# Carrying four partial sums in HBM with GpSimd's accumulating transfers

## The chip, the cores and the metric

One Trainium2 chip, of which the program uses one core. The metric is the time of one execution on the device in microseconds (us). All data are float32.

## What is computed

Eight batch rows of 512 positions by 256 features pass through nine gated feed-forward blocks (eight experts with weights Wg, Wu, Wd and one shared block Sg, Su, Sd, each 256 to 1024 and back), and their weighted sum is added to the input:

```python
g = jnp.einsum('bsd,edf->ebsf', h, Wg)
u = jnp.einsum('bsd,edf->ebsf', h, Wu)
expert_outs = jnp.einsum('ebsf,efd->ebsd', jax.nn.silu(g) * u, Wd)
expert_output = jnp.einsum('be,ebsd->bsd', gating_probs, expert_outs)
shared = jnp.einsum('bsf,fd->bsd', jax.nn.silu(h @ Sg) * (h @ Su), Sd)
return x + (1.0 - sg) * expert_output + sg * shared
```

## The kernel before, in words

The work is cut into 36 units: two halves of the batch (four batch rows each), nine blocks e, and two groups g of 512 hidden features. A unit holds four tiles of 128 hidden features and four batch rows, and forms all 16 products (feature tile by batch row) of the gate, of the up-projection and, after them, of the down-projection. It does this with fewer matmuls than the plain way by a scheme of sums and differences of the four indices: `PAIRS` lists the six pairs (i, j), and for each pair the kernel builds differences and sums of weights (tiles u and wb, on GpSimd, lines 427 to 443) and of inputs (v and b, loaded from copies in HBM, lines 334 and 351).

A unit has two stretches. In the first, the hub, the four products with i = j are made (P and Q steps, lines 503 to 540); in the second, the block, the six pairs (R1 and R steps, lines 549 to 571). Each product ends in `finish` (line 487): ScalarE applies Silu to the gate, VectorE multiplies by the up-projection and the block's weight into a tile h. Tiles h live in a ring of 11 buffers.

The down-projection of a unit (`down`, line 605) is a generator that starts near the end of the unit's hub and runs on into the hub of the next unit; its matmuls are threaded between the gate and up matmuls by the strings at lines 907 to 913. It makes:

- for each pair p the products r (line 664), s or S (lines 672 to 679) and X (line 692). The pairs in `OWN` (0 to 3) have a sum of their own, S, which is carried over all units of a half, in the SBUF tile accS. `carried` (line 639) copies accS into the PSUM bank (`seeded`, line 633), lets TensorE accumulate the unit's matmul on top, and copies the bank back (line 642). Both copies are ScalarE's.
- at the unit that closes a half, no copy back: the seeded bank itself is subtracted from the result's accumulators (lines 674 to 681).
- four products p of row sums (tile rows) and four products q of column sums (tile cols). These sums of h are made by `add_sum` (line 589) on GpSimd: 32 parts a unit, of which the first of a sum adds two tiles, so 24 additions of 128x512 a unit. They are queued by pair in `h_sums` and given out one or two a step, in the block and in the next unit's hub; `flush_sums` (line 597) gives out what is missing just before the matmul that needs it.

The order of the instructions on TensorE and on GpSimd is that of the program text (`manual_schedule`, line 945); on ScalarE, VectorE and SyncE a scheduler sets it. Every engine runs its instructions in order. All DMA transfers are issued by SyncE, except the first loads, which ScalarE issues; GpSimd issues none. In units 2 to 17 a further generator, `prepare` (line 247), makes the second half's input forms: its subtractions and additions on GpSimd are lines 282 to 288 (tile f).

Of the kernel before, what the change touches and what calls it, by code (L numbers as in the profile page):

```python
# [10 lines left out]
F32 = mybir.dt.float32  # L11
AF = mybir.ActivationFunctionType
ALU = mybir.AluOpType
# [4 lines left out]
def kernel(  # L18
# [37 lines left out]
    nc = tc.nc  # L56
    B, S, D = x.shape
    E, _, F = Wg.shape
    P = 128
# [6 lines left out]
    PAIRS = ((1, 0), (0, 2), (3, 0), (1, 2), (3, 1), (3, 2))  # L66
# [17 lines left out]
    zpool = ctx.enter_context(tc.tile_pool(name="z", bufs=6))  # L84
    spool = ctx.enter_context(tc.tile_pool(name="s", bufs=4))
    dpool = ctx.enter_context(tc.tile_pool(name="d", bufs=2))
    iopool = ctx.enter_context(tc.tile_pool(name="io", bufs=2))
    dram = ctx.enter_context(
        tc.tile_pool(name="dram", bufs=1, space=bass.MemoryType.DRAM)
# [7 lines left out]
    gp = nc.gpsimd  # L97
# [25 lines left out]
    def issue_after(later, *first):  # L123

        for at in first:
            tc.add_manual_dep(
                later.ins,
                at.ins.name,
                mybir.DependencyInfo(
                    mybir.DependencyClass.NoSync, mybir.DependencyReason.DATA  # L130
                ),
                reason="issue order",
            )
# [6 lines left out]
    xdram = {}  # L140
    recent = {}
    latest_h = []

# [4 lines left out]
    def new_po(name, turns=False):  # L150

        k = po_next[0]
        if held[k]:
            k = 1 - k
        if not turns:
            po_next[0] = 1 - k
        return ps_o.tile([P, S], F32, tag=f"po{k}", name=name), k
# [223 lines left out]
    for h in range(NH):  # L381
        for e in range(NE):
            for g in range(GRP):
                u = Unit()
# [204 lines left out]
    def add_sum(u):  # L589
        which, n, at = u.sums.pop(0)  # L590
        sums = getattr(u, which)
        first = n not in sums
        if first:
            sums[n] = sumpool.tile([P, S], F32, tag="sum", name=f"{which}{n}_{u.name}")
        gp.tensor_tensor(sums[n], u.h_[n, n] if first else sums[n], u.h_[at], ALU.add)  # L595

    def flush_sums(u, which, n):
        while any(w == which and k == n for w, k, _ in u.sums):
            add_sum(u)

    def closes(u):

        return u.n + (2 if u.h + 1 == NH else 1) == len(units) * (u.h + 1) // NH

    def down(u, acc):

        def tile_of(key):
            acc[key] = apool.tile(
                [P, S], F32, tag=f"acc{key[0]}{key[1]}", name=f"acc{key[0]}{key[1]}_{u.h}"
            )  # L610
            return acc[key]

        def put(key, bank, s):

            if key not in acc:
                if s == 1.0:
                    nc.scalar.copy(tile_of(key), bank)
                else:
                    nc.scalar.mul(tile_of(key), bank, s)
            elif s == 1.0:  # L620
                return ve.tensor_add(acc[key], bank, acc[key])  # L621
            elif s == -1.0:
                return ve.tensor_sub(acc[key], acc[key], bank)
            else:
                return ve.scalar_tensor_tensor(acc[key], bank, s, acc[key], ALU.mult, ALU.add)

        def seeded(key, w, b):

            po, k = new_po(f"{key[0]}{key[1]}_{u.name}")
            full = key in acc and not turned[k]  # L630
            turned[k] = False
            if full:
                nc.scalar.copy(po, acc[key])  # L633
            nc.tensor.matmul(  # L634
                po, w, b, start=not full, stop=True, skip_group_check=full
            )
            return po, full

        def carried(key, w, b):
            po, full = seeded(key, w, b)  # L640
            if full:
                nc.scalar.copy(acc[key], po)
            else:
                put(key, po, 1.0)
            return po if full else acc[key]

        def carried_with(key, w, b, half, s):
            po, full = seeded(key, w, b)
            assert full
            ve.scalar_tensor_tensor(  # L650
                acc[key], xhub[u.h, key[1]][:, half], s, po, ALU.mult, ALU.add
            )

        def single(key, w, b):
            po, k = new_po(f"{key[0]}{key[1]}_{u.name}")
            turned[k] = False
            nc.tensor.matmul(po, w, b, start=True, stop=True)  # L657
            return po, k

        def pair(p):  # L660
            i, j = PAIRS[p]
            d = CI[i] - CI[j]
            def first():
                A, k = single(("r", p), u.Wd[p][i], u.h_[i, j])
                put(("B", j), A, 1.0)
                held[k] = True
                return A, k

            def second():
                args = u.Wd[p][j], u.h_[j, i]  # L670
                if p in OWN and not closes(u):
                    carried(("S", p), *args)
                    return
                if p in OWN:
                    o, full = seeded(("S", p), *args)
                    if not full:
                        ve.tensor_add(o, o, acc["S", p])
                else:
                    o, _ = single(("s", p), *args)
                put(("B", i), o, -1.0)  # L680
                put(("V", p), o, -1.0)

            if closes(u) and p < SWAPPED:
                second()
                yield
                A, k = first()
            else:
                A, k = first()
                yield
                second()  # L690
            yield
            nc.tensor.matmul(  # L692
                A, u.Ud[p], u.X[p], start=False, stop=True, skip_group_check=True
            )
            if closes(u):
                made = ve.tensor_add(A, A, acc["V", p])
                if latest_h[0] is u:
                    issue_after(made, latest_h[1])
                u.puts = put(("b", i), A, 1.0 / d), put(("b", j), A, -1.0 / d)
            else:  # L700
                put(("V", p), A, 1.0)
            held[k] = False
            po_next[0] = 1 - k
            yield

        done = {}
        for what in (0, 1, 2, 3, 4, "p0", "q0", 5, "q1", "p1", "q2", "p2", "q3", "p3"):
            if isinstance(what, int):
                yield from pair(what)
                continue  # L710
            i = int(what[1])
            extra = carry_on.get(u.n)
            if extra is not None and extra[0] == what:
                flush_sums(u, "rows" if what[0] == "p" else "cols", i)
                if what[0] == "p":
                    key, w, b = ("b", i), u.raw_d[:, i, 0:P], u.rows[i]
                else:
                    key, w, b = ("B", i), u.ad[i], u.cols[i]
                carried_with(key, w, b, *extra[1:])
            elif what[0] == "p":  # L720
                flush_sums(u, "rows", i)
                done[what] = carried(("b", i), u.raw_d[:, i, 0:P], u.rows[i])
            else:
                flush_sums(u, "cols", i)
                po, _ = single(("q", i), u.ad[i], u.cols[i])
                put(("B", i), po, 1.0)
                done[what] = po
            if closes(u) and f"p{i}" in done and f"q{i}" in done:
                if CI[i] != 0.0:
                    put(("B", i), done[f"p{i}"], -CI[i])  # L730
                for r in (0, 1):
                    ends[u.h, i, r] = acc["bB"[r], i]
            yield
# [78 lines left out]
    def gate_up(u, nxt):  # L812
# [12 lines left out]
        if u.n == 1:  # L825
            for _ in range(2):
                add_sum(units[0])
# [138 lines left out]
    behind, acc, ahead = iter(()), {}, prepare(1)  # L966
    for u in units:
# [6 lines left out]
        for what in FIRST if u.n == 0 else LAST if nxt is None else OPENING if u.opens else ORDER:  # L974
            if what == "G":
                if nG == TAKE:
                    for _ in behind:
                        pass
                    if u.opens:
                        acc = {}  # L980
                    behind = down(u, acc) if nxt is not None else iter(())
# [7 lines left out]
                if nG > TAKE and nG % 2 == 0 and u.sums:  # L989
                    add_sum(u)  # L990
# [67 lines left out]
```

## Time and profile before

| | us |
|---|---|
| two runs, median (lowest to highest) | 2430.32 (2429.84 to 2430.8) |
| span of the profiled execution | 2427.7 |
| TensorE busy in it (share) | 2423.2 (100%) |
| GpSimd busy in it (share) | 2082.6 (86%) |
| VectorE busy in it (share) | 1919.5 (79%) |
| ScalarE busy in it (share) | 1239.0 (51%) |

Runs take 2.6 us more than the span of the profiled execution (2430.3 against 2427.7), which lies around the instructions of the program. In the rows, PE is TensorE's matmul, PEld its weight load, DVE VectorE, ACT ScalarE, POOL GpSimd and SP SyncE, with a q for the engine's own queue. A float32 matmul stands as two records, so that the timeline merges it as "x2". A row of the timeline gives the start, the length, engine, line, operation, written and read tiles; in square brackets the time that the engine had been idle, and what ended it. An issued DMA is not counted as busy time.

### The profile page before, as it was taken

Reading aid. Unit: us, or ns where it says so; the run is one execution under the profiler, and the core shown is the slowest. Engines: PE = TensorE matmul, PEld = TensorE weight load, DVE = VectorE, ACT = ScalarE, POOL = GpSimd, SP = SyncE. Lnnn points to the kernel's source line nnn. Section 1 sums busy time; section 2 is a strip of 40 time slices with the busy share of each in tenths; the row PEclk is TensorE's granted clock in tenths of the full one; section 3 lists DMA queues with packets and bytes.
Section 4 is the critical chain, followed back from the end, with each engine's and each line's share of the span. In section 5 each row is a group of like instructions: output and inputs, shape, how many; then the busy total and the mean of one; then the engine's idle time right before and its main releaser. Section 6 shows DMA issues by size and latency. Waiting matters only on the chain.

```text
span 2427.7 us, 22771 instructions
## 1 busy us (share of the span) xinstructions
PE 2423.2 (100%) x5735; PEld 1085.3 (45%) x5735; DVE 1919.5 (79%) x2861; ACT 1239.0 (51%) x2294; POOL 2082.6 (86%) x2321
## 2 busy tenths in 40 slices
PE   9999999999999999999999999999999999999999
PEld 4444444444444444444444444444444444444446
DVE  8788888777777877787987777777877777777795
ACT  5555555554555454555455555555455555555542
POOL 7988888898988989898888888888888888888882
PEclk9999999999999999999999999999999999999999
DMA  4333333334333332334453322322333333323245
GB/s 161 108 111 107 110 98 100 117 117 126 104 122 104 103 113 94 108 112 124 119 124 110 91 84 91 92 87 90 100 104 104 95 97 90 92 87 96 79 132 145
DMA packets 221201, 257.92 MB, mean 106 GB/s; under 512 B 64016, under 2 KB 156432, under 8 KB 221072
## 3 DMA queue, kind: packets, MB, share of 16 engines
q1 hardware_dynamic: 220240, 256.17, 35.4%
q8 instruction: 48, 0.79, 0.1%
q14 instruction: 81, 0.66, 0.1%
q10 hardware_dynamic: 832, 0.30, 0.0%
HBM read 238.59 MB, written 17.83 MB: 106 GB/s over the span
## 4 chain that ended last, share of the span: by engine, by line
PE 100%; DVE 0%; issue 0%
PE c L565 31%; PE c L552 15%; PE c L530 10%; PE c L506 10%; PE r L657 7%; PE r L692 7%; PE b L634 5%; PE S L634 5%; PE q L657 5%; PE s L657 2%; PE tail L792 1%; PE B L634 0%; PE ptx L234 0%; PE touchg L372 0%; PE c L212 0%; PE ptx L208 0%
## 5 line engine op out<-in xcount | busy, mean ns | idle before, releaser
L565 PE MATMUL c<-b,wb 128*128 128x512 f32 x1728 | 847.1, 592 | 0.0
L490 ACT ACTIVATE sg<-c 128x512 f32<-128x512 f32 x576 | 343.7, 597 | 571.1 <-DVE c L570 330.3
L495 DVE SCALAR_TENSOR_TENSOR h<-sg,coef,c 128x512 f32<-128x512 f32 x576 | 427.5, 742 | 240.7 <-PE c L565 133.9
L565 PEld LDWEIGHTS c<-b,wb 128*128 128x128 f32 x1728 | 328.2, 190 | 408.8 <-issue 388.2
L552 PE MATMUL c<-v,u 128*128 128x512 f32 x864 | 441.1, 592 | 0.0
L595 POOL TENSOR_TENSOR rows<-rows,h 128x512 f32<-128x512 f32 x280 | 369.4, 1319 | 0.0
L557 DVE TENSOR_TENSOR c<-D,c 128x512 f32<-128x512 f32 x432 | 298.8, 692 | 76.7 <-ACT sg L490 57.9
L595 POOL TENSOR_TENSOR cols<-cols,h 128x512 f32<-128x512 f32 x280 | 358.8, 1281 | 0.0
L570 DVE TENSOR_TENSOR c<-c,D 128x512 f32<-128x512 f32 x432 | 298.6, 691 | 21.7 <-PE c L565 21.2
L506 PE MATMUL c<-x,w 128*128 128x512 f32 x572 | 274.5, 592 | 0.0
L442 POOL TENSOR_TENSOR wb<-u,wb 128x256 f32<-128x256 f32 x108 | 79.5, 736 | 220.1 <-ACT wb L440 220.1
L552 PEld LDWEIGHTS c<-v,u 128*128 128x128 f32 x864 | 163.6, 190 | 206.1 <-issue 164.8
L657 PE MATMUL r<-h,wd 128*128 128x512 f32 x420 | 214.5, 592 | 0.0
L692 PE MATMUL r<-X,ud 128*128 128x512 f32 x420 | 214.5, 592 | 0.0
L530 PE MATMUL c<-x,at 128*128 128x512 f32 x432 | 208.7, 592 | 0.0
L540 ACT COPY D<-c 128x512 f32<-128x512 f32 x284 | 165.6, 584 | 84.1 <-DVE h L495 84.1
L581 DVE TENSOR_TENSOR X<-h,h 128x512 f32<-128x512 f32 x202 | 199.4, 987 | 6.8
L595 POOL TENSOR_TENSOR rows<-h,h 128x512 f32<-128x512 f32 x140 | 193.4, 1382 | 0.0
L595 POOL TENSOR_TENSOR cols<-h,h 128x512 f32<-128x512 f32 x140 | 180.5, 1289 | 0.0
L512 ACT COPY P<-c 128x512 f32<-128x512 f32 x216 | 126.1, 586 | 105.5 <-PE c L506 100.9
L506 PEld LDWEIGHTS c<-x,w 128*128 128x128 f32 x572 | 108.5, 190 | 135.8 <-issue 112.4
L633 ACT COPY S<-accS 128x512 f32<-128x512 f32 x132 | 77.9, 590 | 158.4 <-DVE accV L621 140.2
(115 smaller groups left out, 3470.5 us busy)
## 6 DMA issues: line engine op xcount, KB each, us to landing
b<-xs SPq DMA_DIRECT2D x210, 512.0 KB, 3.6
v<-xs SPq DMA_DIRECT2D x210, 256.0 KB, 2.6
wd<-in_L_cond_Wd_dram SPq DMA_DIRECT2D x32, 512.0 KB, 4.8
w<-in_L_cond_Wg_dram SPq DMA_DIRECT2D x127, 128.0 KB, 3.5
w<-in_L_cond_Wu_dram SPq DMA_DIRECT2D x127, 128.0 KB, 3.6
f<-xd SPq DMA_DIRECT2D x12, 512.0 KB, 5.3
xs<-f SPq DMA_DIRECT2D x18, 256.0 KB, 2.7
xin<-in_x_dram SPq DMA_DIRECT2D x16, 256.0 KB, 3.7
```

The costliest lines, as they stand in the source:

```text
L490: nc.scalar.activation(s, bank, AF.Silu)
L495: made = ve.scalar_tensor_tensor(t, u.sg[i, j], coef[:, u.e, b : b + 1], bank, ALU.mult, ALU.mult)
L506: nc.tensor.matmul(bank, u.raw[i][:, m, 0], xhub[u.h, i][:, 0], start=True, stop=True)
L530: nc.tensor.matmul(bank, u.at[i][:, m], xhub[u.h, i][:, 1], start=False, stop=True, skip_group_check=True,)
L552: nc.tensor.matmul(bank, u.U[p][:, m], u.V[p], start=False, stop=True, skip_group_check=True)
L557: made = ve.tensor_sub(other, u.Ds[j, m], bank)
L565: nc.tensor.matmul(bank, u.W[p][:, r, m], u.VB[p][:, r], start=False, stop=True, skip_group_check=True,)
L570: first_order(u, ve.tensor_add(bank, bank, u.Ds[j, m]), "add", p, m)
L595: gp.tensor_tensor(sums[n], u.h_[n, n] if first else sums[n], u.h_[at], ALU.add)
L634: nc.tensor.matmul(po, w, b, start=not full, stop=True, skip_group_check=full)
L657: nc.tensor.matmul(po, w, b, start=True, stop=True)
L692: nc.tensor.matmul(A, u.Ud[p], u.X[p], start=False, stop=True, skip_group_check=True)
```

## The change

Two things change, both on GpSimd's queue.

First, S of the pairs 0 to 3 is no longer carried in SBUF. The matmul starts its bank afresh, ScalarE copies the bank into a staging tile St (a ring of four), and a transfer adds it to a tile S in HBM: the first of a half is a plain store from SyncE, the others are transfers of GpSimd with `accum_op=ALU.add`, 256 KB each. The transfer is not issued at once but when the next of these sums is made (`parked`). In the unit that closes a half, each sum is loaded back into a staging tile, Sin, by SyncE, and seeds the bank as accS did.

Second, of the 24 additions of `add_sum` two become such transfers in SBUF: the additions of h to the row sums 1 and 2 at pair 3, in all units but the first.

```diff
+    stpool = ctx.enter_context(tc.tile_pool(name="st", bufs=4))
...
+        if not first and which == "rows" and at in (PAIRS[3], PAIRS[3][::-1]) and u.n:
+            gp.dma_start(sums[n], u.h_[at], accum_op=ALU.add)
+            return
         gp.tensor_tensor(sums[n], u.h_[n, n] if first else sums[n], u.h_[at], ALU.add)
...
+        def flush_hbm():
+
+            while parked:
+                to, t, opening = parked.pop(0)
+                if opening:
+                    nc.sync.dma_start(to, t)
+                else:
+                    gp.dma_start(to, t, accum_op=ALU.add)
+
+        def to_hbm(p, w, b):
+
+            flush_hbm()
+            po, _ = single(("S", p), w, b)
+            t = stpool.tile([P, S], F32, tag="st", name=f"St{p}_{u.name}")
+            nc.scalar.copy(t, po)
+            opening = (u.h, p) not in hbm
+            if opening:
+                hbm[u.h, p] = dram.tile([P, S], F32, tag=f"S{u.h}_{p}", name=f"S{u.h}_{p}")
+            parked.append((hbm[u.h, p], t, opening))
...
                 if p in OWN and not closes(u):
-                    carried(("S", p), *args)
+                    to_hbm(p, *args)
                     return
                 if p in OWN:
+                    flush_hbm()
+                    acc["S", p] = stpool.tile([P, S], F32, tag="st", name=f"Sin{p}_{u.h}")
+                    nc.sync.dma_start(acc["S", p], hbm[u.h, p])
                     o, full = seeded(("S", p), *args)
```

The instructions of TensorE and VectorE and their order stay as they are. ScalarE loses 124 copies (2299 rows become 2175), GpSimd gains 124 transfers and has 68 more in place of additions (2319 rows become 2443), SyncE gains 16 transfers.

GpSimd's queue at the end of the block of unit 8_0 (half 0, block 8, group 0), before. The tile names carry the index of the sum or pair first, then half, block and group; h12 is the product of feature tile 1 and batch row 2.

```order
L595 TENSOR_TENSOR cols0_0_8_0_8152<-cols0_0_8_0_8152,h30_0_8_0_8209 128x512
L595 TENSOR_TENSOR rows0_0_8_0_8172<-rows0_0_8_0_8172,h03_0_8_0_8213 128x512
L595 TENSOR_TENSOR cols3_0_8_0_8320<-h33_0_8_0_8065,h03_0_8_0_8213 128x512
L595 TENSOR_TENSOR rows1_0_8_0_8139<-rows1_0_8_0_8139,h12_0_8_0_8259 128x512
L595 TENSOR_TENSOR cols2_0_8_0_8224<-cols2_0_8_0_8224,h12_0_8_0_8259 128x512
L595 TENSOR_TENSOR rows2_0_8_0_8244<-rows2_0_8_0_8244,h21_0_8_0_8263 128x512
L430 TENSOR_TENSOR u0_8_1_0_8363<-at0_8_1_1_8229,w0_8_1_0_8178 128x256
```

The same place now:

```order
L601 TENSOR_TENSOR cols0_0_8_0_8223<-cols0_0_8_0_8223,h30_0_8_0_8281 128x512
L673 DMA S0_2_601<-St2_0_8_0_8328 128x512
L601 TENSOR_TENSOR rows0_0_8_0_8243<-rows0_0_8_0_8243,h03_0_8_0_8285 128x512
L601 TENSOR_TENSOR cols3_0_8_0_8394<-h33_0_8_0_8135,h03_0_8_0_8285 128x512
L599 DMA rows1_0_8_0_8209<-h12_0_8_0_8332 128x512
L601 TENSOR_TENSOR cols2_0_8_0_8296<-cols2_0_8_0_8296,h12_0_8_0_8332 128x512
L599 DMA rows2_0_8_0_8316<-h21_0_8_0_8336 128x512
L433 TENSOR_TENSOR u0_8_1_0_8437<-at0_8_1_1_8301,w0_8_1_0_8249 128x256
```

One transfer of S has come in between two additions, and two additions have become transfers; the forms u and wb of the next unit queue behind them. The other three transfers of a unit stand in the same way: S3 of the unit before after the block's first addition, then S0 and S1 some 7 to 9 us apart.

SyncE's queue ahead of the block of unit 8_1, which closes the first half, before:

```order
L402 DMA w1_0_0_0_8659<-in_L0_cond_Wg_dram 128x2x128
L402 DMA w1_0_0_0_8659<-in_L0_cond_Wu_dram 128x2x128
L334 DMA v0_8_1_2_8386<-xs0_2_428 128x512
L351 DMA b0_8_1_0_8380<-xs0_0_285 128x1024
L351 DMA b0_8_1_1_8384<-xs0_1_377 128x1024
```

And now:

```order
L405 DMA w1_0_0_0_8736<-in_L0_cond_Wu_dram 128x2x128
L337 DMA v0_8_1_2_8460<-xs0_2_431 128x512
L703 DMA Sin0_0_8685<-S0_0_471 128x512
L703 DMA Sin1_0_8749<-S0_1_538 128x512
L703 DMA Sin2_0_8804<-S0_2_601 128x512
L354 DMA b0_8_1_0_8454<-xs0_0_288 128x1024
L354 DMA b0_8_1_1_8458<-xs0_1_380 128x1024
```

Three of the four loads of the sums stand ahead of two loads of b; the third of them reads S2, whose last addition is the transfer shown on GpSimd's queue above.

More of the change, by code (lines that the diff above doesn't have):

```diff
@@ L142 @@
     latest_h = []
+    hbm = {}
+    parked = []
     turned = [False, False]
```

## The prediction

> **What bounds the kernel now.** I read first the page's head and its chain, to see which engine sets the end.
>
> ```profile
> span 2427.7 us, 22771 instructions
> PE 2423.2 (100%) x5735; PEld 1085.3 (45%) x5735; DVE 1919.5 (79%) x2861; ACT 1239.0 (51%) x2294; POOL 2082.6 (86%) x2321
> PE 100%; DVE 0%; issue 0%
> ```
>
> TensorE is busy 2423.2 of 2427.7 us, and the chain that ended last lies on it alone. Everything else is hidden. So work that is taken off another engine can give back at most 2427.7 - 2423.2 = 4.5 us, and the question is whether the change makes TensorE wait. It adds its work to GpSimd (POOL), so I read next how that engine's stretches look, unit by unit. A unit lasts 67.0 us.
>
> ```profile
> 1033.00:1100.00 67.00, 67.00 (x158) 29.68 (x157) 53.02 (x80) 34.52 (x64) 61.67 (x68) 1.00 0.35 106
> 1100.00:1167.00 67.00, 67.00 (x158) 29.67 (x157) 52.60 (x80) 35.08 (x65) 57.57 (x64) 1.00 0.40 118
> ```
>
> The columns are PE, PEld, DVE, ACT and POOL busy, the clock, the DMA share and the rate. In the first window, where `prepare` runs its f steps, GpSimd has 67.00 - 61.67 = 5.33 us to spare in a unit; in the second 9.43. That is the room for new work, if it lies in the right places.
>
> **What is taken away.** Two groups of copies on ScalarE and 68 additions on GpSimd:
>
> ```profile
> L633 ACT COPY S<-accS 128x512 f32<-128x512 f32 x132 | 77.9, 590 | 158.4 <-DVE accV L621 140.2 <-DVE accV L623 14.2 <-DVE accb L650 2.1
> L642 ACT COPY accS<-S 128x512 f32<-128x512 f32 x124 | 71.8, 579 | 0.0
> L595 POOL TENSOR_TENSOR rows<-rows,h 128x512 f32<-128x512 f32 x280 | 369.4, 1319 | 0.0
> ```
>
> Of the 132 seeds 8 stay; 124 go, 124 x 0.59 = 73 us of ScalarE, which was 51% busy beside a full TensorE. The copy back becomes the copy into St, at the same place and price. This is worth nothing on the path (bound 4.5 us, above). The additions are 68 x 1.32 = 90 us of GpSimd.
>
> **What is added on GpSimd** is the issue of 192 transfers, 124 + 68. The trace has no transfer issued by GpSimd, so the price of one, I, is unknown, and nearly all hangs on it. The nearest rows:
>
> ```profile
> 1107.79 0.34 SPq L351 DMA_DIRECT2D b<-xs  x1
> L463 POOL TENSOR_SCALAR a<-wd 128x512 f32<-128x512 f32 x35 | 21.6, 618 | 0.0
> v<-xs SPq DMA_DIRECT2D x210, 256.0 KB, 2.6
> b<-xs SPq DMA_DIRECT2D x210, 512.0 KB, 3.6
> ```
>
> Below, I could be the 0.34 us for which SyncE's queue is held by an issue; above, 2.6 us, the time to the landing of a 256 KB transfer, if the engine stayed with it to the end. Between them stand GpSimd's own passes over a tile of this shape: 0.62 us with one operand, 1.32 with two. A transfer that adds has two ends to be addressed for 128 rows each, so I take the row of the two-operand pass as nearest and, as no data pass through the engine, a tenth less: I = 1.2 us. Both ends are kept for the range.
>
> The Trainium skill, "DMA: Bandwidth & Descriptors", section Specifications, puts the first byte of a transfer from GpSimd's software path at about 1 us and of one from SyncE's at about 0.6. The issue row of 0.34 us does not contradict the second; no row here shows the first. By I = 1.0 the sum below would come to no loss at all.
>
> **Where the lateness goes.** Each issue pushes back all of GpSimd's later instructions; each of its idle gaps takes some of it back. I followed the unit with f steps, from the first gap on:
>
> ```profile
> 1033.66 0.73 POOL L442 TENSOR_TENSOR wb<-u,wb 128x256 f32<-128x256 f32 x1 [2.30 <-ACT wb L440]
> 1037.98 1.27 POOL L595 TENSOR_TENSOR rows<-h,h 128x512 f32<-128x512 f32 x1
> 1041.39 0.72 POOL L442 TENSOR_TENSOR wb<-u,wb 128x256 f32<-128x256 f32 x1 [0.91 <-ACT wb L440]
> 1056.91 0.73 POOL L442 TENSOR_TENSOR wb<-u,wb 128x256 f32<-128x256 f32 x1 [0.64 <-ACT wb L440]
> 1064.33 1.27 POOL L595 TENSOR_TENSOR rows<-rows,h 128x512 f32<-128x512 f32 x1
> 1066.79 1.72 POOL L595 TENSOR_TENSOR rows<-rows,h 128x512 f32<-128x512 f32 x1
> 1071.86 0.73 POOL L442 TENSOR_TENSOR wb<-u,w 128x256 f32<-128x256 f32 x1 [0.48 <-PE c L565]
> 1089.44 1.27 POOL L595 TENSOR_TENSOR cols<-cols,h 128x512 f32<-128x512 f32 x1
> 1092.14 1.02 PE L657 MATMUL q<-cols,ad 128*128 128x512 f32 x2
> ```
>
> S3 is issued behind the row at 1037.98: late by I, less the gap of 0.91 at 1041.39. S0 and S1 add 2I, the gap at 1056.91 takes 0.64, S2 adds I. The two additions at 1064.33 and 1066.79 go (1.27 + 1.72 = 3.0) and two issues come. The gap at 1071.86 takes 0.48. No gap follows until the next block. In this stretch the column sum at 1089.44 is the tightest: it ends at 1090.71, and TensorE starts the matmul q that reads it at 1092.14, so 1.43 us of lateness is free. What is left reaches TensorE: 6I - 0.91 - 0.64 - 3.0 - 0.48 - 1.43 = 6I - 6.46, which at I = 1.2 is 0.74 us.
>
> In a unit without f steps the gaps are larger:
>
> ```profile
> 1108.40 0.72 POOL L442 TENSOR_TENSOR wb<-u,wb 128x256 f32<-128x256 f32 x1 [2.78 <-ACT wb L440]
> 1115.57 0.73 POOL L442 TENSOR_TENSOR wb<-u,w 128x256 f32<-128x256 f32 x1 [0.92 <-PE c L565]
> 1123.86 0.73 POOL L442 TENSOR_TENSOR wb<-u,wb 128x256 f32<-128x256 f32 x1 [2.04 <-ACT wb L440]
> 1138.81 0.73 POOL L442 TENSOR_TENSOR wb<-u,w 128x256 f32<-128x256 f32 x1 [0.47 <-PE c L565]
> L282 POOL TENSOR_TENSOR f<-f,f 128x512 f32<-128x512 f32 x6 | 7.7, 1276 | 0.0
> ```
>
> 2.78 us takes S3 whole; 0.92 and 2.04 take S0 and S1 up to I = 1.48; S2 and the two row transfers are left, against 3.0 us of additions and 0.47 of gap: 3I - 3.47, 0.13 us at I = 1.2, inside the 1.43. Nothing is lost. Above I = 1.48 it is 5I - 7.86, above zero from I = 1.57.
>
> Six groups of f steps (the last row) make about seven units of the first kind, the closing one of the first half with its shifted work counted in; some 28 are of the second. **The sum**: 7 x 0.74 + 28 x 0 = 5 us; 2427.7 + 5 = 2433 us of span, and with the 2.6 us that runs take beyond it, 2436 us. GpSimd would be held 2082.6 - 90 + 192 x 1.2 = 2223 us of it.
>
> **Waits that the change adds**, each costed at nothing, with its cover:
>
> ```profile
> 1083.29 1.28 POOL L595 TENSOR_TENSOR rows<-rows,h 128x512 f32<-128x512 f32 x1
> 1106.35 0.58 ACT L642 COPY accS<-S 128x512 f32<-128x512 f32 x1
> 1113.37 1.27 POOL L595 TENSOR_TENSOR rows<-rows,h 128x512 f32<-128x512 f32 x1
> 1117.04 1.02 PE L565 MATMUL c<-b,wb 128*128 128x512 f32 x2
> 1128.39 0.34 SPq L334 DMA_DIRECT2D v<-xs  x1
> 1128.84 1.27 POOL L595 TENSOR_TENSOR rows<-rows,h 128x512 f32<-128x512 f32 x1
> 1160.81 1.02 PE L565 MATMUL c<-b,wb 128*128 128x512 f32 x2
> 1166.03 0.59 ACT L633 COPY S<-accS 128x512 f32<-128x512 f32 x1 [0.49 <-DVE accB L650]
> ```
>
> GpSimd waits for the copy into St before it issues S0; the copy ended at 1106.93, and the issue stands where GpSimd was at 1113.37 (ahead of that row), 6.4 us later, since it is parked for a pair. Uncovered, the forms wb behind it would be late by as much. The additions to rows 1 and 2 that follow the transfers wait for their landing; the first stands at 1083.29, 19 us after the addition at 1064.33 that becomes a transfer, against a landing of 2.6. A St buffer and an HBM tile come back a whole unit later. VectorE's h waits for the landing of the row transfers, a ring of 11 tiles on; 16 tiles take 67 us, so it is tens of us on.
>
> In the closing units SyncE loads Sin0 to Sin2 behind the v of 1128.39; Sin2 has to wait until S2, issued on GpSimd at 1128.84 and by then a few us late, has landed, so about 1135; the three loads and the b behind them come some 6 us later than now. That b is first read at 1160.81, the sum at 1166.03; both have 20 us and more. With this cover gone, each of eight loads would cost 2.6 us, 21 us together.
>
> **Rivals.** *The issue is dear* (slower). If I lies above 1.57, every unit loses at the same column sum: loss = 28 x (5I - 7.86) + 7 x (6I - 6.46). It passes 2% (48.6 us) at I = 1.71. At I = 2.0 it is 60 + 39 = 99 us, 2529 us in all; at the bound of 2.6 it is 144 + 64 = 208 us, 2638. For it: an adding transfer may need more set-up than any row here shows, and GpSimd is the busiest engine but one. Against it: the engine moves no data, and a two-operand pass over the same rows costs 1.32.
>
> *The relief of ScalarE pays* (a little faster): the seeds waited 158.4 us for VectorE, and they are gone. Against it: TensorE is at 67.00 of 67.00 in both windows. At most 2430.3 - 4.5 = 2426 us; it needs I at or under 1.07, where 6I - 6.46 is zero.
>
> *The transfers crowd the loads* (slower): b is issued at 1107.79, as soon as its buffer is free, and read at 1117.04, so of 9.25 us its 3.6 us of landing leave 5.6. Six more transfers of 256 KB in 67 us come on a DMA share of 0.35 to 0.40. Landing would have to reach 9.25 us before TensorE waits; 1 us more on each of 210 loads is 210 us, 2640 us. v is issued two pairs ahead and has more.
>
> *The change does not lighten anything*: should GpSimd have to wait at each issue until the one before has landed, that is the first rival at its upper end.
>
> **How the numbers follow.** The forecast (I between 1.07 and 1.71) gets 0.67, the relief 0.10, the dear issue 0.20, the crowded loads 0.03. The predicted time is 2436 us. The low end is 2424 us, the relief with its 4.5 us and a little for the spread of runs; the high end follows from I = 1.9, 28 x 1.64 + 7 x 4.94 = 80 us, so 2510 us; what lies above it I put at 0.15. A measurement of this kernel tells about 2% from no change: faster by that is excluded by the 4.5 us, 0.01; within it 0.76; slower 0.23.
>
> **What would show it right or wrong.** Right: TensorE's share stays at 100%, a window of one unit is still 67.0 us or up to 68 in units with f steps, and GpSimd's gaps before wb shrink by what the issues take. I itself is read from the stretch between two additions with an issue between. The step on the column sums is wrong if TensorE waits elsewhere than at q, above all at wb. The prediction is wrong as a whole if GpSimd has no gaps left and the units are longer than 68.3 us throughout: then the issue is dear; if TensorE waits for b or v, the loads are crowded.

## The result and the profile after

The changed kernel takes 2458.4 us (median of two runs, 2457.97 to 2458.84), against 2430.3 before: 28 us or 1.2% slower, ratio 1.0116 with a 95% interval of 1.0087 to 1.0146. That is inside the predicted range and 22 us above the predicted 2436. As the traces below show, it did not come about in the way that was predicted.

The page of the profiled execution, its head and its chain:

```profile
span 2456.2 us, 23071 instructions
PE 2435.0 (99%) x5735; PEld 1087.3 (44%) x5735; DVE 1963.3 (80%) x2861; ACT 1166.3 (47%) x2170; POOL 2155.3 (88%) x2445
PE 95%; POOL 2%; DVE 2%; issue 1%; DMA 0%; ACTq 0%; SPq 0%; DVEq 0%; POOLq 0%
```

The span has grown by 28.5 us. TensorE is busy 11.8 us longer with the same 5735 instructions (2435.0 against 2423.2), so some of its matmuls run slower; and the time in which it isn't busy has grown from 4.5 to 21.2 us, by 16.7. The two make up the 28.5. VectorE, whose program hasn't changed, is busy 44 us longer. GpSimd and VectorE now have a share in the chain.

What TensorE waited for, as the view of waits has it (engine, line, what it waited for: us in total, times, longest):

```profile
PE r L721 <- DVE accB L627: 14.3, 5, 3.8
```

Five waits, all at the matmul r that reads an X tile. The next entry of the view is 1.6 us. Before, the longest entry of this view was 1.0 us. The groups of X on VectorE (X is the difference of two tiles h, both in SBUF), first of the kernel before, then of the changed one, with the two new groups of GpSimd:

```profile
L581 DVE TENSOR_TENSOR X<-h,h 128x512 f32<-128x512 f32 x202 | 199.4, 987 | 6.8
```

```profile
L584 DVE TENSOR_TENSOR X<-h,h 128x512 f32<-128x512 f32 x202 | 248.5, 1230 | 6.7
L673 POOL DMA_DIRECT2D S<-St x124 | 109.4, 882 | 0.0
L599 POOL DMA_DIRECT2D rows<-h x68 | 88.9, 1307 | 0.0
```

The 202 X cost 49 us more, and the other large groups of VectorE are as they were (the largest, h, 427.5 us both times). Five of the X account for more than half of the 49 us: the X of the third pair (pair 2) in units 1, 7, 10, 12 and 15, counted from 0, takes 6.22, 7.03, 7.62, 5.81 and 6.97 us, where before none took over 1.86. Four more take 2.2 to 4.3 us, and no wait of TensorE at r follows them. Four of the five units have f steps; unit 1 has none, but gives out two parts of the sums a step, as units 18 and 19 do too, where others give out one.

One of the five in full, the unit around 1070 us. GpSimd first, then VectorE, then TensorE:

```profile
1069.20 0.87 POOL L673 DMA_DIRECT2D S<-St  x1
1069.81 1.56 POOL L601 TENSOR_TENSOR rows<-rows,h 128x512 f32<-128x512 f32 x1
1071.05 1.00 POOL L445 TENSOR_TENSOR wb<-u,w 128x256 f32<-128x256 f32 x1
...
1076.75 1.14 POOL L673 DMA_DIRECT2D S<-St  x1
1077.36 1.82 POOL L601 TENSOR_TENSOR cols<-cols,h 128x512 f32<-128x512 f32 x1
1083.77 0.72 POOL L445 TENSOR_TENSOR wb<-u,wb 128x256 f32<-128x256 f32 x1 [4.59 <-ACT wb L443]
```

```profile
1072.77 6.97 DVE L584 TENSOR_TENSOR X<-h,h 128x512 f32<-128x512 f32 x1
...
1080.26 0.68 DVE L627 TENSOR_TENSOR accB<-r,accB 128x512 f32<-128x512 f32 x1
```

```profile
1081.00 2.08 PE L721 MATMUL r<-X,ud 128*128 128x512 f32 x2 [3.11 <-DVE accB L627]
1082.90 2.05 PE L555 MATMUL c<-v,u 128*128 128x512 f32 x2
1084.74 1.91 PE L568 MATMUL c<-b,wb 128*128 128x512 f32 x2
1086.44 1.27 PE L663 MATMUL r<-h,wd 128*128 128x512 f32 x2
1087.55 1.02 PE L568 MATMUL c<-b,wb 128*128 128x512 f32 x2
```

Three things are to be seen. The issue of S0 at 1069.20 holds GpSimd until 1069.81, 0.61 us; that, and not 1.2, is the price I that the prediction looked for. Behind it GpSimd runs without a pause to 1079.18, and by the lengths shown each of its instructions still runs when the next has begun: the row addition that takes 1.27 us elsewhere shows 1.56, the form wb 1.00 in place of 0.73. And the X that VectorE starts in this stretch ends 0.56 us after the stretch does (1079.74 against 1079.18). VectorE runs in order, so the accB addition two places behind X is late as well, and with it the matmul r, which starts 0.06 us after it. Once it starts, TensorE's next four pairs of matmuls take 2.08, 2.05, 1.91 and 1.27 us in place of 1.02; 3.2 us more together. Such pairs follow four of the five waits (2.35, 3.17, 3.75 and 3.11 us). Behind the fifth, of 1.94 us, the pairs take 1.13 and 1.10 us. All five together make 10 of the 11.8 us of longer busy time.

In four of the five units X ends like this. In unit 1 it doesn't:

```profile
114.89 6.22 DVE L584 TENSOR_TENSOR X<-h,h 128x512 f32<-128x512 f32 x1
```

```profile
119.87 1.12 POOL L673 DMA_DIRECT2D S<-St  x1
```

X ends at 121.11, 0.6 us behind the slot of the next issue (119.87 to 120.48, when GpSimd's next addition starts), while GpSimd pauses only at 122.28. So a later issue can let an X in too; the one at 1076.75 above did not.

The same X in the kernel before, and GpSimd's instruction beside it, in a stretch that is just as full:

```profile
1051.14 0.86 DVE L581 TENSOR_TENSOR X<-h,h 128x512 f32<-128x512 f32 x1
```

```profile
1051.41 1.72 POOL L595 TENSOR_TENSOR cols<-h,h 128x512 f32<-128x512 f32 x1
```

There X and GpSimd took turns: X took 0.86 us, and GpSimd's addition 0.45 longer than its usual 1.27. Back-to-back work on GpSimd alone doesn't keep X out.

Windows, of one unit's slow spot and of a whole unit of the other kind (columns as in the prediction: PE, PEld, DVE, ACT, POOL busy, clock, DMA share, GB/s):

```profile
1072.00:1090.00 18.00, 14.89 (x28) 5.96 (x27) 15.61 (x15) 5.09 (x10) 13.41 (x15) 0.81 0.56 153
1109.00:1176.00 67.00, 67.00 (x158) 29.67 (x157) 52.98 (x80) 31.65 (x59) 60.09 (x69) 1.00 0.55 138
```

In the slow spot the granted clock is 0.81. The Trainium skill, "TensorE: Matmul & The Clock Gate", Part 1, states that an idle window of some 3.4 us puts the clock at half rate, and that about as long a busy window brings it back. The trace agrees in kind: behind a wait of 3.11 us a matmul pair takes 2.08 us, twice 1.02, and the full rate is back 6.5 us after the wait. It doesn't agree in size: in unit 1 a wait of 2.35 us, with a second of 0.78 behind the next pair, was enough for pairs of 1.95 and 1.91 us. The other unit is as it was, TensorE 67.00 of 67.00.

### The profile page after: what moved, and what is told of

It reads as the page before. It is cut to its first block, busy times and chain, and to the rows that moved or that the text cites. A ratio compares the mean times of both kernels' runs of the same rounds, so it can differ in the third digit from the quotient of the medians.

```text
span 2456.2 us, 23071 instructions
## 1 busy us (share of the span) xinstructions
PE 2435.0 (99%) x5735; PEld 1087.3 (44%) x5735; DVE 1963.3 (80%) x2861; ACT 1166.3 (47%) x2170; POOL 2155.3 (88%) x2445
## 4 chain that ended last, share of the span: by engine, by line
PE 95%; POOL 2%; DVE 2%; issue 1%; DMA 0%; ACTq 0%; SPq 0%; DVEq 0%; POOLq 0%
PE c L568 29%; PE c L555 15%; PE c L533 10%; PE c L509 10%; PE r L721 7%; PE r L663 7%; PE b L640 5%; PE q L663 5%; PE S L663 4%; PE s L663 2%; PE tail L821 1%; DVE X L584 1%; POOL rows L601 1%; POOL cols L601 0%; DVE h L498 0%
## 5 line engine op out<-in xcount | busy, mean ns | idle before, releaser
L498 DVE SCALAR_TENSOR_TENSOR h<-sg,coef,c 128x512 f32<-128x512 f32 x576 | 427.5, 742 | 233.2 <-PE c L568 141.8
L601 POOL TENSOR_TENSOR cols<-cols,h 128x512 f32<-128x512 f32 x280 | 387.3, 1383 | 0.0
L601 POOL TENSOR_TENSOR rows<-rows,h 128x512 f32<-128x512 f32 x212 | 288.1, 1359 | 0.0
L584 DVE TENSOR_TENSOR X<-h,h 128x512 f32<-128x512 f32 x202 | 248.5, 1230 | 6.7
L721 PE MATMUL r<-X,ud 128*128 128x512 f32 x420 | 217.5, 600 | 14.3 <-DVE accB L627 14.3
L601 POOL TENSOR_TENSOR cols<-h,h 128x512 f32<-128x512 f32 x140 | 197.8, 1413 | 0.0
L550 ACT COPY c<-P 128x512 f32<-128x512 f32 x216 | 127.5, 590 | 46.3 <-DVE h L498 42.9
```

Source lines behind the costliest of these rows:

```text
L498: made = ve.scalar_tensor_tensor(t, u.sg[i, j], coef[:, u.e, b : b + 1], bank, ALU.mult, ALU.mult)
L584: made = (gp if closes(u) and p in (1, 2, 3, 4) else ve).tensor_tensor(u.X[p], u.h_[j, i], u.h_[i, j], ALU.subtract)
L721: nc.tensor.matmul(A, u.Ud[p], u.X[p], start=False, stop=True, skip_group_check=True)
```

## The experiments

The theory after these traces, the **lock-out**: an issue on GpSimd puts that engine into a state in which an X on VectorE can't get in, until GpSimd goes idle or waits for itself. Rivals: the traffic of the new transfers, GpSimd simply being too full, and the late GpSimd of the prediction, with waits at q. The later expectations use letters, and each says what its letter stands for; A is the lock-out throughout. All times are medians against runs of the kernel before on the same chip (2430.0 to 2430.2 us).

**Which part does it.** Only the sums in HBM, with the row additions kept on GpSimd:

```diff
-        if not first and which == "rows" and at in (PAIRS[3], PAIRS[3][::-1]) and u.n:
-            gp.dma_start(sums[n], u.h_[at], accum_op=ALU.add)
-            return
```

> The change with the HBM sums alone; the two row transfers a unit are additions again. Lock theory (behind a transfer that GpSimd issues, its next instructions overlap until it idles, and a VectorE subtraction X with both inputs in SBUF cannot start in that stretch): the five long X of 5.8 to 7.6 us come behind the issues of S0 and S1, so they stay, and the time is 2448 to 2462 us. Traffic theory (the transfers' own data slow X or the loads): two thirds of the bytes are left, so two thirds of the 28 us, 2446 to 2451 us, with many X slowed a little rather than a few slowed much. Late-GpSimd theory (the recorded one: issues push the column sums back): GpSimd has 2 x 0.7 us more a unit than the change, so the loss is larger, 2460 to 2475 us, with waits at q.

Measured: 2460.6 us, ratio 1.0124 (1.0109 to 1.0139). The same five X take 6.22, 7.02, 7.62, 5.82 and 6.95 us, and the view of waits has TensorE at r for 14.9 us, in 7 waits. In 24 units the X of pair 4 now takes 3.5 to 3.9 us as well. In the changed kernel row transfers are issued there, and the X takes about 1.4 us, which is a second sign that a later issue can let an X in. No wait of TensorE follows these.

Only the row transfers, with the sums carried in SBUF as before:

```diff
-                    to_hbm(p, *args)
+                    carried(("S", p), *args)
```

> The kernel before with the two row transfers a unit alone; S is carried as before. Lock theory: the stretch behind the row issues is short (it ended at the next gap in the trace of the change, X of at most 4.3 us with no wait of TensorE behind it), so 2428 to 2434 us. Traffic theory: a third of the 28 us, 2437 to 2441 us. Late-GpSimd theory: the issue is shorter than the addition, so no loss, 2428 to 2432 us.

Measured: 2430.6 us, ratio 1.0001 (0.9992 to 1.0011); one X of 3.88 us, and no wait of TensorE at r. The whole loss belongs to the transfers of S.

**The traffic or the issue.** The same transfers as plain copies, issued by GpSimd in the one kernel and by SyncE in the other (`gp.dma_start(to, t)` and `nc.sync.dma_start(to, t)`, and the same for the rows):

> The change with plain copies in place of the adding transfers, issued by GpSimd at the same places (the sums of S and two parts of the row sums are left out: each copy overwrites). Lock theory: the issue matters, not what the transfer does, so the five long X stay, 2448 to 2462 us. Traffic theory: the adding transfer reads its target too, so with plain copies a good part of the loss goes, 2436 to 2446 us.

> The same plain copies, of the same bytes to the same places, issued by SyncE instead of GpSimd (the sums of S and two parts of the row sums are left out). Lock theory: GpSimd issues nothing, so no X over 2.5 us and no loss, 2427 to 2434 us. Traffic theory: the same as with GpSimd's plain copies, 2436 to 2456 us.

Measured: from GpSimd 2449.1 us, ratio 1.0080 (1.0065 to 1.0095); from SyncE 2430.2, ratio 1.0001 (0.9991 to 1.0011), with no X over 2 us. The traffic falls as a cause: the same bytes between the same places cost nothing when SyncE issues them. From GpSimd:

```profile
1061.08 0.56 POOL L673 DMA_DIRECT2D S<-St  x1
1061.66 1.28 POOL L601 TENSOR_TENSOR rows<-rows,h 128x512 f32<-128x512 f32 x1
```

```profile
1064.65 6.34 DVE L584 TENSOR_TENSOR X<-h,h 128x512 f32<-128x512 f32 x1
```

A plain issue shows 0.3 us less, and the additions behind it overlap hardly more than usual (1.28 against 1.27); yet four X of pair 2 take 5.2 to 7.0 us (that of unit 1 is free here, 1.10 us). So the visible overlap is a mark of the adding transfer, and X is kept out without it.

**The issue or the fullness.** Copies by SyncE, and at each former issue on GpSimd an addition of 128x128 and one of 128x8, as long as an issue (`occupy`); and the same with a transfer of 8 elements issued by GpSimd at that place:

```diff
-                    gp.dma_start(to, t, accum_op=ALU.add)
+                    nc.sync.dma_start(to, t)
+                    occupy(t)
```

> Edit: the changed kernel with the same transfers issued by SyncE as plain copies (the sums are left out), and in the place of each former issue on GpSimd an addition of 128x128 and one of 128x8, together about 0.6 us, as long as the slot of an issue. Theory A (it is the issue on GpSimd that locks the X addition out): no X over 3 us, no wait of TensorE, 2427 to 2434 us. Theory C (GpSimd is simply too full, and 0.6 us of any work at these places shuts the gaps in which X ran): long X and waits at r<-X as in the changed kernel, 2443 to 2465 us.

> Edit: the changed kernel with the same transfers issued by SyncE as plain copies (the sums are left out), and in the place of each former issue on GpSimd a transfer of 1 partition of 8 elements. Theory A in its simple form (any issue on GpSimd locks the X addition out until GpSimd's next idle time, whatever it moves): long X of 5 to 7 us as with the plain copies issued by GpSimd, 2443 to 2452 us. Theory D (the lock-out goes with the work of writing the descriptors of 128 rows): no X over 3 us, 2428 to 2434 us; and the issue itself takes clearly less than the 0.57 us of a plain copy of 128 rows.

Measured: with the additions 2430.0 us, ratio 1.0000 (0.9991 to 1.0010); with the small transfers 2449.1, ratio 1.0082 (1.0067 to 1.0097). The group of X in the first of the two:

```profile
L590 DVE TENSOR_TENSOR X<-h,h 128x512 f32<-128x512 f32 x202 | 203.0, 1005 | 6.7
```

and in the second one of GpSimd's issues with the X that follows:

```profile
1066.01 0.54 POOL L103 DMA_DIRECT2D tiny<-St  x1
```

```profile
1069.56 6.33 DVE L594 TENSOR_TENSOR X<-h,h 128x512 f32<-128x512 f32 x1
```

Fullness falls with the first: the same GpSimd time in the same places, as ordinary additions, costs nothing, though it keeps GpSimd busier than the plain issues do (2110 against 2090 us). The size of the transfer falls with the second: 32 bytes keep X out as 256 KB do. Their issue takes 0.55 us on the mean against 0.57, so what GpSimd does in an issue is not less here, and no run shows which part of it matters. It is the fact of an issue on GpSimd, not the bytes that it moves.

**Two ways around that failed.** The X of pair 2 put on GpSimd in the five units, so that VectorE has none to be kept out:

```diff
-        made = (gp if closes(u) and p in (1, 2, 3, 4) else ve).tensor_tensor(
+        made = (gp if closes(u) and p in (1, 2, 3, 4) or p == 2 and u.n in (1, 7, 10, 12, 15) else ve).tensor_tensor(
```

> The change with one more edit: in the five units whose X of pair 2 was locked out (units 1, 7, 10, 12 and 15 in program order) that subtraction is made by GpSimd, which cannot be locked out by itself. Lock theory: the five waits of TensorE before the X matmul go, though GpSimd has 1.3 us more in each of these units: 2429 to 2438 us. Traffic theory: the subtraction is slow on whichever engine has it, 2445 us or more. Late-GpSimd theory: more work on GpSimd, more loss, 2460 us or more.

and the issues put just ahead of the forms wb of pairs 2, 3 and 5, where GpSimd mostly waits:

```diff
+    def flush_hbm():
...
+            flush_hbm()
...
-            flush_hbm()
```

> The change with the transfers of S issued at other places: just ahead of the additions that build wb for pairs 2, 3 and 5, where GpSimd waits for ScalarE in most units. Same transfers, same bytes, same number. Lock theory: the idle time behind the issue ends the overlap, so no X over 3 us ahead of a wait of TensorE, 2429 to 2438 us; if GpSimd has no gap left in the units with f steps, a part of the five stays. Traffic theory: as the change, 2450 to 2460 us. Late-GpSimd theory: issue time is the same, so as the change, 2450 to 2460 us.

Measured: 2485.6 us, ratio 1.0229 (1.0212 to 1.0246), and 2507.3, ratio 1.0316 (1.0300 to 1.0331). Both were expected near 2430, and both made it worse. With X on GpSimd the wait for the X of pair 2 was gone, and with it the idle time that it had given to GpSimd behind the next issue, of S1 (4.59 us, at 1083.77 above); the X of pair 3 was kept out instead, for 11.2 to 13.6 us; TensorE's waits at r came to 43.0 us in 6. With the issue ahead of wb, GpSimd waits for ScalarE's copy before the issue (39 times), and no idle time is left behind it; TensorE's waits at r came to 47.2 us in 14:

```profile
881.16 0.89 POOL L443 DMA_DIRECT2D S<-St  x1 [4.43 <-ACT St L680]
```

```profile
882.36 12.88 DVE L594 TENSOR_TENSOR X<-h,h 128x512 f32<-128x512 f32 x1
```

The expectations had taken the place of the X for the cause. Any X that falls into a stretch in which GpSimd runs on behind an issue can pay.

**What ends it.** Behind each adding transfer two additions of 128x8, of which the second reads the first, so that GpSimd has to wait for itself; and as a control two that read neither:

```diff
+    def settle():
+        nc.gpsimd.tensor_tensor(ticks[0], ident[:, 0:8], ident[:, 0:8], ALU.add)
+        nc.gpsimd.tensor_tensor(ticks[1], ticks[0], ticks[0], ALU.add)
...
                     gp.dma_start(to, t, accum_op=ALU.add)
+                    settle()
```

> Edit: the changed kernel, and behind each of GpSimd's adding transfers two GpSimd additions of 128x8, the second of which reads what the first wrote, so that GpSimd waits for itself right behind each issue; some 0.5 us more of GpSimd per issue. Theory A (behind an issue GpSimd takes its next instructions before the last has ended, and the X addition stays locked out until GpSimd once waits for its own result): X of pair 2 stays under 3 us in all units, the five waits at r<-X go, 2429 to 2437 us. Theory B (the X addition gets in only when GpSimd goes idle, whatever stands behind the issue): the five X of 6 to 8 us stay, stretches are a little longer, 2456 to 2475 us. Theory C (an issue simply takes GpSimd time that the chain needs): waits at wb or q, over 2475 us.

> Edit: the changed kernel, and behind each of GpSimd's adding transfers two GpSimd additions of 128x8 of which neither reads what the other wrote: the same instructions as in the kernel that waits for itself (2443 us), without the wait. Theory A (it is the wait of GpSimd for its own result that lets the X addition in): the X additions of 5 to 8 us stay, waits begin at r<-X, 2456 to 2475 us. Rival E (two more small instructions or 0.3 us of distance behind the issue are enough): no X over 2 us, waits only at q and B, 2438 to 2446 us.

Measured: with the wait 2443.4 us, ratio 1.0053 (1.0036 to 1.0070), and no X over 2 us; without it 2470.0, ratio 1.0165 (1.0149 to 1.0180), with X of up to 8.22 us. With the wait, GpSimd and VectorE around one issue:

```profile
1067.99 0.85 POOL L680 DMA_DIRECT2D S<-St  x1
1068.60 0.48 POOL L99 TENSOR_TENSOR tick<-ident 128x8 f32<-128x8 f32 x1
1069.15 0.20 POOL L100 TENSOR_TENSOR tick<-tick 128x8 f32<-128x8 f32 x1
1069.31 1.27 POOL L608 TENSOR_TENSOR cols<-cols,h 128x512 f32<-128x512 f32 x1
```

```profile
1070.11 1.02 DVE L590 TENSOR_TENSOR X<-h,h 128x512 f32<-128x512 f32 x1
```

and without:

```profile
729.52 0.88 POOL L682 DMA_DIRECT2D S<-St  x1
730.15 0.64 POOL L102 TENSOR_TENSOR tick<-ident 128x8 f32<-128x8 f32 x2
730.47 1.53 POOL L610 TENSOR_TENSOR rows<-rows,h 128x512 f32<-128x512 f32 x1
```

```profile
732.46 8.22 DVE L592 TENSOR_TENSOR X<-h,h 128x512 f32<-128x512 f32 x1
```

In the first the second small addition starts 0.07 us after the first has ended, and from there on everything is as before the issue: the column addition takes 1.27 us, X gets in. In the second the same two instructions stand without a wait, the row addition still shows 1.53, and X is kept out. So it is the wait that lets X in, and not the two instructions. The wait shows in the starts too: the first small addition holds the queue for 0.55 us, where both together take 0.32 without it. Theory B of the first expectation, that X gets in only when GpSimd goes idle, isn't refuted by this: what failed is its forecast that the long X stay. A wait for itself leaves GpSimd idle as well, if only for 0.07 us, and no run tells the two apart. Of all the X over 1.9 us in these kernels none outlasts by more than 0.57 us a pause of GpSimd that falls into it; but well over half of them end ahead of any pause, most of these within 1 us behind the slot of a later issue, as 58 of the 63 in the kernel without the wait do. So of the lock-out it is shown that an issue brings it about and that a pause ends it, but not that only a pause does. The number expected of the first, 2429 to 2437 us, was missed: the 13 us that stay are another loss, which the view of waits names:

```profile
PE q L670 <- POOL cols L608: 6.8, 7, 1.9
PE B L647 <- POOL cols L608: 1.9, 1, 1.9
```

That is the loss of the prediction, at q, since an issue with its two additions now holds GpSimd for 1.32 us (1067.99 to 1069.31).

To have the cure without that price, the two additions were put behind the issue of S0 alone:

```diff
                     gp.dma_start(to, t, accum_op=ALU.add)
+                    if p == 0:
+                        settle()
```

> Edit: the changed kernel with the two additions of 128x8, the second reading the first, behind the issue of the sum of pair 0 alone, the one that stands ahead of the long X additions: once per unit in place of 12 times in the kernel that waits for itself behind every issue. Theory A: the five long X go as they do there, and the 0.5 us of GpSimd is paid once per unit, so that the waits at q go as well: 2429 to 2436 us. Rival (other issues lock X out too once the first is settled, or 0.5 us shifts the next stretch onto an X): X of over 3 us elsewhere, 2440 to 2456 us.

Measured: 2481.5 us, ratio 1.0212 (1.0197 to 1.0227), far above both bounds. (A unit has up to six issues on GpSimd, not the twelve that the expectation counts.) The X of pair 2 go free (at most 1.8 us), and in six units the X of pair 3, behind the next issue, of S1, is kept out for 6.9 to 12.4 us:

```profile
1098.17 0.84 POOL L679 DMA_DIRECT2D S<-St  x1
1098.78 1.54 POOL L607 TENSOR_TENSOR cols<-cols,h 128x512 f32<-128x512 f32 x1
...
1105.10 1.80 POOL L607 TENSOR_TENSOR rows<-rows,h 128x512 f32<-128x512 f32 x1
...
1108.15 2.11 POOL L607 TENSOR_TENSOR cols<-cols,h 128x512 f32<-128x512 f32 x1
...
1109.98 1.89 POOL L439 TENSOR_TENSOR u<-at,w 128x256 f32<-128x256 f32 x1
1111.95 0.73 POOL L451 TENSOR_TENSOR wb<-u,w 128x256 f32<-128x256 f32 x1
```

```profile
1100.72 10.53 DVE L590 TENSOR_TENSOR X<-h,h 128x512 f32<-128x512 f32 x1
```

As in the kernel with X on GpSimd, the idle time behind S1's issue is gone with the wait at r. X ends at 1111.25, within the last instruction (the form u of 1109.98, which shows 1.89 us in place of 0.72) before GpSimd's next pause, of 0.08 us, at 1111.87. What let it in ahead of that pause isn't shown. The rows show the state growing: a full-width addition shows 1.54 us behind the first adding transfer, 1.80 behind the second, 2.11 behind the third, where 1.27 is usual, while the next instruction starts no later. Behind the pause, at 1111.95, all is usual again.

**Why just these units.** The two additions of each f step left out:

```diff
-            gp.tensor_tensor(B_j, v, B_j, ALU.add)
...
-            gp.tensor_tensor(B_i, v, B_i, ALU.add)
```

> Edit: the changed kernel without GpSimd's two additions per pair of the f steps (the stored forms of the x products, B_j and B_i, then hold the loaded values: this part of the computation is left out). In four of the five units one of these stands in the stretch behind the issue of the sum of pair 0. Theory A: in these units the stretch is 1.2 us shorter or is broken by an idle, X ends as much sooner, and each loses 1 to 5.4 us less; the unit without f steps keeps its X of 6.2 us and its loss: 2432 to 2452 us. Rival F (the f steps have no part in it, the units differ in something else): the four X keep 5.8 to 7.6 us, 2454 to 2460 us.

Measured: 2440.2 us, ratio 1.0044 (1.0027 to 1.0060). Three of the four X in units with f steps are back at 0.69 us, unit 1 keeps 6.29, as expected, and unit 10 has 6.41. Where the X is free, one sees why:

```profile
1056.00 0.87 POOL L671 DMA_DIRECT2D S<-St  x1
1056.62 1.56 POOL L599 TENSOR_TENSOR rows<-rows,h 128x512 f32<-128x512 f32 x1
1058.28 0.73 POOL L443 TENSOR_TENSOR wb<-u,w 128x256 f32<-128x256 f32 x1
```

```profile
1060.80 0.69 DVE L582 TENSOR_TENSOR X<-h,h 128x512 f32<-128x512 f32 x1
```

The row addition ends at 1058.18 and the form wb starts at 1058.28. A pause of 0.10 us before wb is enough; from start to start, wb comes 1.66 us behind the addition, where it came 1.24 behind it in the changed kernel (1069.81 to 1071.05). In units without f steps wb waited for TensorE at this place before the change (0.92 us, at 1115.57), as it most likely does here; when GpSimd comes to it late by an f step, as at 1071.05 above, it no longer has to wait, and the pause is gone. In unit 10 wb follows without a pause even so. There the subtraction and the scaling of its f step, which this kernel keeps, still stand ahead of the issue, 1.27 and 0.94 us at 712.89 and 714.25, and that they make GpSimd late enough is the likely reason.

## Why the prediction was right or wrong

**TensorE bounds, no gain is to be had: right.** With the same copies and the transfers on SyncE the time is 2430.2 us, although ScalarE has 73 us less to do (1166.1 against 1239.0). The relief was worth nothing.

**The issue price I: too high.** 0.61 us from the start of an issue to the next instruction, where 1.2 was taken from the two-operand pass. By its own formulas that is no loss anywhere, 2430 us. (The I at which its dear issue passes 2% comes to 1.72 by them, not to 1.71.)

**The loss at the matmul q, 5 us in seven units: it didn't occur.** TensorE never waited there for long in the changed kernel. But the working of the gaps held up where it could be tried: with the wait behind each issue, an issue costs 1.32 us, and 7 x (6 x 1.32 - 6.46) = 10 us. TensorE then waited seven times at q, in six units, and once at B for a column sum, 8.7 us in all, near the sum and mostly at its place. Matmuls slowed by 4.3 us in all made up most of the rest of the 13.9 us that the span was longer than before, and these the sum doesn't have.

**"Against it: the engine moves no data": the step that failed.** The prediction took an issue for time on GpSimd's queue and nothing else, and followed only what is queued behind it there. What it costs is on VectorE, in instructions that the change doesn't touch: an X with both inputs in SBUF, which before had to take turns with GpSimd (0.86 us against 0.45 us longer beside it), is kept out behind an issue for up to 7.62 us. The term that the prediction put at nothing without a reason, a delay of VectorE, came to 16.7 us of TensorE idle and 11.8 of slower matmuls. The rows that showed X and GpSimd taking turns were in the trace of before and were not read for it. That the result lay inside the range, 22 us from 2436, is luck: the range was wide because the issue might have been dear, and it was half as dear as taken. A loss of 5 us that wasn't there stands in the place of one of 28 that was.

**The waits that were costed at nothing: right.** The landing of the adding transfers is longer than the 2.6 us taken, and of the loads a little:

```profile
S<-St POOLq DMA_DIRECT2D x124, 256.0 KB, 4.6
rows<-h POOLq DMA_DIRECT2D x68, 256.0 KB, 5.2
b<-xs SPq DMA_DIRECT2D x210, 512.0 KB, 4.2
```

b came 0.6 us later than before, against the 5.6 it had to spare. No wait of TensorE for b, v, a sum or Sin is in the list. The crowded loads and the dear issue were false.

**The sign named for a wrong step fired:** TensorE waits elsewhere than at q, though not at wb but at r. The unit shown above without a long X is still 67.0 us.

What the mechanism is inside the chip is only argued. The Trainium skill, "SBUF — State Buffer", section Who interferes with whom, says that a VectorE instruction with two SBUF inputs contends with a GpSimd instruction that reads SBUF, since its second input comes through a read port that the two share, and that the lock on the shared ports is exclusive. The X rows agree that there is contention; they also show that a turn isn't had at the end of each instruction, since 6.97 us run across six of GpSimd's. The Trainium skill, "GPSIMD Engine Reference", section 2.1, adds that GpSimd's cores are not held together from one instruction to the next unless something waits for completion. The growing overlap behind each adding transfer (1.54, 1.80, 2.11 us) and its end at a wait agree with cores that have fallen apart, so that there is no moment between two instructions at which none of them reads. That the plain copies keep X out with hardly any overlap to be seen is not explained by this, and no run here looks inside. It also stays open why one later issue lets an X in and another doesn't.

## What to carry to other kernels

Costing an issue on GpSimd by its slot in the queue isn't enough: list the VectorE instructions with two SBUF inputs that can start behind it before GpSimd next goes idle or waits for its own result, and count each of them as possibly late until then (of VectorE's large groups here, X alone is of this kind). If the transfer needn't add, issue it from SyncE, which cost nothing here; if it must, a wait of GpSimd for its own result behind every issue, not only behind the one that hurts, gave VectorE its turns back, for 0.7 us each. Even so the kernel stayed 13 us slower than before. When a wait is cured on one instruction, look for the idle time that this wait had given to others: here two cures of one X moved the loss to the next and made it larger.

## What was not expected of the hardware

- A GpSimd issue of 32 bytes and one of 256 KB take the same 0.55 to 0.57 us; an adding one holds the queue for 0.61 us but shows as 0.87.
- Behind a GpSimd issue a VectorE subtraction of two SBUF tiles took up to 13.6 us in place of 1, while GpSimd's own instructions started no later than they otherwise would.
- A pause of 0.07 to 0.10 us on GpSimd, by the lengths shown, was enough to end it; by the starts, the instruction behind it came 0.4 us later.
- Five waits of TensorE, 14.3 us together, were followed by 10 us more in matmuls, at a granted clock of 0.72 to 0.86 in the 12 us around four of them and of 1.00 around the shortest, of 1.94 us.
